# Writing the padding rows of four stored arrays at other places in the kernel

## Chip, cores and metric

The kernel runs on one core of a Trainium2 chip. The metric is the time of one execution on the device in microseconds (us), taken as the median of several runs; lower is better. Before the change it is 1056.62 us, the median of three runs (1054.39, 1056.62 and 1062.56).

## What is computed

Four graph layers on 2708 nodes with 512 features each; every layer adds its result to its input and normalises the rows. `adj` is a sparse 2708 x 2708 matrix whose first nodes have many neighbours and whose later ones have few. Cut to what matters:

```
# layer 0
d = 1 / sqrt((adj + I).sum(1))
x = layernorm(x + (d[:, None] * (adj + I) * d[None, :]) @ x @ W.T + b)
# layer 1
mask = adj > 0;  head = mask / max(sqrt(row sum of mask), 1e-12);  inc = adj + head
x = layernorm(x + (inc @ x) / row sum of inc)
# layer 2 (adj is both adj_a and adj_b)
h = x @ W_sa;  e = exp(-leaky_relu(s_left + s_right)) where adj != 0, else 0
x_a = (e / (row sum of e + 1e-5)) @ h;  x_b = adj @ (x @ W_gcnb) + b_gcnb
x = layernorm(x + sigmoid(attn_a * x_a + attn_b * x_b))
# layer 3
x = layernorm(x + relu(adj @ (max(sign(x), 0) @ sign(weight).T)))
```

## The kernel before

**Blocks and tiles.** The 2708 rows are cut into 22 blocks of 128 (the last has 20). Block 0, the dense one, is multiplied with all 22 blocks of the matrix. For every other block b the kernel first searches which nodes are its neighbours and packs them into `ROOM[b]` tiles of 128 (107 tiles over all blocks). A list of node numbers, `index[b]`, goes with each tile. A place in a tile that no neighbour fills points to a row behind the real ones: the arrays in device memory have `PAD + P` rows with `PAD = N = 2708`, and rows `PAD` and up must hold zeros.

**Stored arrays.** `y_rows` (layer 0's projected features), `x1_rows` (output of layer 0), `x2_rows` (output of layer 1, the product h, and two score columns; 1026 numbers per row) and `xw_rows` (the sign product, in half precision) live in device memory. Each layer gathers rows of one of them with indirect DMAs that POOL issues: `gathered` (L582, its DMA at L584) and, in layer 2, `gathered_2` (L1723). The score column of the padding rows of `x2_rows` holds a very large number (`MASKED`, 1e30), so that its exponential is zero. In the profile both `x1_rows` and `x2_rows` appear as `x_rows`.

**The start.** The pool `pre` (from L669) holds what only the search needs. SP loads the rows of two blocks (`load`, L685: two halves `arow` from `adj`, four buffers; `load_x`, L693: x and a column of the transposed matrix). Then come ACT's DMAs in this order: the weight `w0` (L703), the padding rows of the four arrays (L708), the second half of the padding rows of `x2_rows` (L712) and the two mask columns (L718). `zero` is a 128 x 128 tile; each padding DMA reads it four times, so that a row of 512 numbers is written in four pieces of 128. POOL makes small constants.

**The search.** `turn(at)` (L1182) takes one block at a time, in the order of the groups `GROUPS`: (1), (2, 3), (4, 5), (6, 7, 8) and so on, and block 0 last. In a turn, ACT sums the rows (`sum_rows`, L761), DVE marks non-zeros (`mark`, L806), PE counts them, and for each complete group DVE, PE and ACT make the list (`count`, `steps_of`, `look_up` with the cast `steps` at L931, `keep_looked` with the copy `look` at L963, `list_nodes` ending at L993 with `row_at`). `fetch` (L1012) then has POOL gather the group's matrix tiles, one indirect DMA for each of 107 tiles (L1014); between some of them a POOL memset `rest` (L1020) lets time pass. Two turns behind, `scale0` (L1052) scales a block of `y` and stores it to `y_rows` on ACT's queue (L1057). In turn `NTURN` (22, after the last block) `count_block0` (L1165) counts block 0's positive entries.

The turns stand inside `with in_order()` (L591, used at L1235): it makes each engine run the instructions traced within it in the order in which they are written. Elsewhere the order on an engine is chosen at build time.

**Layer 0.** The loop at L1401 takes the blocks in `sequence` (0, 1, 21, 2, ..., 20): gathers from `y_rows` (L584 by L1411), products on PE (`add_tile`, its matmul at L1318), a normalisation, and a store to `x1_rows` by SP (L1430). After a turn it runs what the table `between` (L1379) lists for it: loads and columns for layer 2's attention, the signs of the last weight (`signs`, L1352, which loads `w3` on ACT's queue at L1354), counts and roots for layer 1. Layers 1 to 3 follow with gathers from `x1_rows`, `x2_rows` and `xw_rows`.

Of the kernel before, what the change touches and what calls it, by code (L numbers as in the profile page):

```python
# [8 lines left out]
F32 = mybir.dt.float32  # L9
F32R = mybir.dt.float32r  # L10
BF16 = mybir.dt.bfloat16
F16 = mybir.dt.float16
# [7 lines left out]
P = 128  # L20
# [4 lines left out]
MASKED = 1e30  # L25
# [470 lines left out]
def sparse_layers(ctx, tc, x, adj, adj_t, w0_t, b0, w_sa, a_sa, w_gcnb, b_gcnb, wa, ba, wb, bb, w3_t,  # L496
# [11 lines left out]
    nc = tc.nc  # L508
    N, D = x.shape
    KC = D // P  # L510
    NB = -(-N // P)
    PAD = N
    XW = 2 * D + 2
# [12 lines left out]
    const = ctx.enter_context(tc.tile_pool(name="s_const", bufs=1))  # L526
# [18 lines left out]
    y_rows = dram.tile([PAD + P, D], F32, tag="y_rows", name="y_rows")  # L545
    x1_rows = dram.tile([PAD + P, D], F32, tag="x1_rows", name="x1_rows")
    x2_rows = dram.tile([PAD + P, XW], F32, tag="x2_rows", name="x2_rows")
    xw_rows = dram.tile([PAD + P, D], F16, tag="xw_rows", name="xw_rows")
# [24 lines left out]
    dia_pos = const.tile([P, NB], F32, name="s_dia_pos")  # L573
    own0 = const.tile([P, NB], F32, name="s_own0")
    own1 = const.tile([P, NB], F32, name="s_own1")
    head0_row = const.tile([P, P], F32, name="s_head0_row")
    cols = const.tile([P, NB, EXTRA], F32, name="s_cols")

# [90 lines left out]
    with tc.tile_pool(name="s_pre", bufs=1) as pre:  # L669
# [31 lines left out]
            load_x(b)  # L701
        w0 = pre.tile([P, KC, D], F32, name="s_w0")
        nc.scalar.dma_start(w0, w0_t.rearrange("(k p) o -> p k o", p=P))  # L703
        zero = pre.tile([P, D], F32, tag="y", name="s_zero", bufs=3)[:, :P]
        nc.vector.memset(zero, 0.0)
        for d in (y_rows, x1_rows, x2_rows, xw_rows):
            z = zero.bitcast(F16)[:, :P] if d is xw_rows else zero
            nc.scalar.dma_start(  # L708
                d[PAD:, :D].rearrange("p (k i) -> p k i", i=P),
                z[:, None, :].to_broadcast([P, KC, P]),  # L710
            )
        nc.scalar.dma_start(  # L712
            x2_rows[PAD:, D : 2 * D].rearrange("p (k i) -> p k i", i=P),
            zero[:, None, :].to_broadcast([P, KC, P]),
        )
        masked = pre.tile([P, XW - 2 * D], F32, name="s_masked")
        nc.vector.memset(masked, MASKED)
        nc.scalar.dma_start(x2_rows[PAD:, 2 * D :], masked)  # L718

        tri = pre.tile([P, P], F32, name="s_tri")  # L720
        nc.vector.memset(tri, 1.0)
# [65 lines left out]
        def inverse_root(b: int):  # L787
            m = rows(b)
            deg, root_ = degree_of.pop(b)
            return newton_steps(  # L790
                dinv[:m, b : b + 1], deg[:m], root_[:m, 0:1], root_[:m, 1:2], 1
            )
# [76 lines left out]
        def count(g):  # L869
            b0_, G = g[0], len(g)  # L870
            hit = small.tile([P, GM, NB, 2], BF16, tag="hit", name=f"hit{b0_}", bufs=2)
            nc.vector.tensor_scalar(
                hit[:, :G], search[g]["hits"][:, :, :, 0:2], 0.0, None, op0=ALU.is_gt
            )
            kind = small.tile([P, 3, GM * NB], BF16, tag="kind", name=f"kind{b0_}", bufs=2)
            upper, both, lower = (kind[:, c, : G * NB] for c in range(3))
            side = [hit[:, :G, :, c].rearrange("p g s -> p (g s)") for c in range(2)]
            nc.vector.tensor_tensor(both, side[0], side[1], op=ALU.mult)
            nc.vector.tensor_tensor(upper, side[0], both, op=ALU.subtract)
            nc.vector.tensor_tensor(lower, side[1], both, op=ALU.subtract)  # L880
            turn = small.tile([P, 3, GM * NB], F32, tag="turn", name=f"turn{b0_}", bufs=2)
            for c in range(3):
                nc.vector.tensor_tensor_scan(
                    turn[:, c, : G * NB], keep[:, :G].rearrange("p g s -> p (g s)"),
                    kind[:, c, : G * NB], 0.0, op0=ALU.mult, op1=ALU.add,
                )
            turns = turn[:, :, : G * NB].rearrange("p c (g s) -> p c g s", g=G)
            nc.vector.tensor_copy(found[:, :, b0_ : b0_ + G], turns[:, :, :, NB - 1])
            table = small.tile([P, 3 * GM, NT], BF16, tag="table", name=f"table{b0_}", bufs=2)
            nc.vector.tensor_tensor(  # L890
                table[:, : 3 * G, :NB].rearrange("p (c g) s -> p c g s", c=3), turns,
                kind[:, :, : G * NB].rearrange("p c (g s) -> p c g s", g=G), op=ALU.mult,
            )
            nc.vector.tensor_copy(table[:, : 3 * G, NB + 2], lane[:, : 3 * G])
            search[g].update(table=table)
# [269 lines left out]
        def count_block0():  # L1165

            for h, ar in enumerate(arows.pop(0)):
                nc.vector.tensor_scalar(
                    ar, ar, 0.0, 0.0, op0=ALU.is_gt, op1=ALU.add, accum_out=counts0[:, h : h + 1]
                )  # L1170
# [7 lines left out]
        def each(action, at: int):  # L1178
            if 0 <= at < NTURN:
                action(arrival[at])  # L1180

        def turn(at: int):  # L1182
            step_of = {at - last_at[g]: g for g in GROUPS[1:]}

            def chain(action, since: int):
                if step_of.get(since, SOON) != SOON:
                    action(step_of[since])

            each(degree, at - 1)
            each(root, at - 1)  # L1190
            each(own_diagonal, at - 1)
            chain(steps_of, 2)
            each(sum_rows, at)
            steps = inverse_root(arrival[at - 1]) if 0 < at <= NTURN else []
            found_in = step_of.get(1)

            def count_found():
                count(found_in)
                count_partitions(found_in)

            if found_in:
                steps.insert(0, count_found)
            if at < NTURN and arrival[at]:
                mark(arrival[at], steps)
            else:
                for step_ in steps:
                    step_()
            if found_in == SOON:
                steps_of(SOON)
            each(load_x, at + 2)  # L1210
            each(load, at + 2)
            each(transpose_x, at)
            each(keep_transposed, at)
            chain(look_up, 2)
            chain(list_nodes, 3)
            if found_in == SOON:
                look_up(SOON)
                keep_looked(SOON)
            if at == 0:
                for step_ in (  # L1220
                    count, count_partitions, steps_of, look_up, keep_looked, list_nodes
                ):
                    step_(GROUPS[0])
            each(scale0, at - 2)
            each(project0, at - 1)
            chain(keep_looked, 2)
            each(fold, at - 3)
            each(grow0, at - 3)
            if found_in == SOON:
                list_nodes(SOON)  # L1230
            fetch(len(to_fetch))
            if at == NTURN:
                count_block0()

        with in_order():  # L1235
            for at in range(NTURN + 4):
                turn(at)
# [87 lines left out]
    with tc.tile_pool(name="s_l0", bufs=10, reuse_waits="tile") as lp:  # L1325
# [14 lines left out]
        def attention_columns(s: int):  # L1340
            for k in range(KC):
                scr = lp.tile([P, D], F32, tag="scr", name=f"scr{s}_{k}", bufs=1)
                nc.vector.scalar_tensor_tensor(
                    scr, wsa[:, k, :D], 1.0, a_row[:, s, :], op0=ALU.mult, op1=ALU.mult,
                    accum_out=vec[:, s, k : k + 1],
                )
# [5 lines left out]
        def signs(k: int):  # L1352
            w3 = work.tile([P, D], F32, tag="xb", name=f"s_w3_{k}")
            nc.scalar.dma_start(w3, w3_t[k * P : (k + 1) * P, :])  # L1354
            neg = lp.tile([P, D], F32, tag="scr", name=f"s_neg{k}", bufs=1)
            nc.vector.tensor_scalar(neg, w3, 0.0, None, op0=ALU.is_lt)
            nc.vector.scalar_tensor_tensor(
                bw[:, k, :], w3, 0.0, neg, op0=ALU.is_gt, op1=ALU.subtract
            )
# [4 lines left out]
        def grow1(j: int):  # L1364
# [12 lines left out]
            grown1.append(j)  # L1377

        between = {  # L1379
            2: [attention_loads], 4: [lambda: attention_columns(0)],  # L1380
            5: [lambda: attention_columns(1)], 6: [attention_sides],
            8: [lambda: signs(0)], 10: [lambda: signs(1)], 12: [lambda: signs(2)],
            14: [lambda: signs(3)],
        }
# [124 lines left out]
    with tc.tile_pool(name="s_l1", bufs=8, reuse_waits="tile") as lp:  # L1509
# [67 lines left out]
        for at, b in enumerate(sequence):  # L1577
            m = rows(b)
            if b:
# [8 lines left out]
                for i0, n, (r0, r1) in runs_of(b, 3):  # L1588
# [4 lines left out]
                        name=f"inc{b}_{i0}", bufs=4 if half else 3,  # L1593
# [323 lines left out]
    with tc.tile_pool(name="s_l3", bufs=11, reuse_waits="tile") as lp, \  # L1917
# [92 lines left out]
        for at, b in enumerate(order3):  # L2010
# [21 lines left out]
            for i0 in range(0, tiles(b), CH3):  # L2032
                n = min(CH3, tiles(b) - i0)
                p = halves_of(
                    packed[b][:, i0 : i0 + n, :].rearrange("p n i -> p (n i)"), P, n * m,
                    f"{b}_{i0}",
                )
# [94 lines left out]
```

## Time and profile before

The profiled execution took 1000.5 us; its span, from the first instruction to the last, is 998.8 us. The median of the runs shown is 1056.62 us.

| engine | busy us | share of the span | instructions |
|---|---|---|---|
| PE (matmul) | 875.6 | 88% | 3775 |
| DVE | 657.8 | 66% | 2571 |
| POOL | 549.6 | 55% | 580 |
| PEld (weight load) | 458.8 | 46% | 3793 |
| ACT | 386.5 | 39% | 821 |

By stretch, from the busy times of each engine in each:

| us from the start | PE busy | DVE busy | ACT busy | POOL busy | DMA share | GB/s |
|---|---|---|---|---|---|---|
| 0 to 12 | 1.45 | 4.80 | 0.00 | 2.79 | 0.85 | 276 |
| 12 to 24 | 2.50 | 4.68 | 6.54 | 0.00 | 1.11 | 262 |
| 24 to 44 | 16.01 | 15.77 | 12.21 | 13.24 | 1.03 | 388 |
| 100 to 140 | 37.51 | 38.17 | 26.74 | 34.41 | 0.98 | 332 |
| 140 to 165 | 23.89 | 23.23 | 12.60 | 20.94 | 0.50 | 149 |
| 165 to 195 | 7.21 | 14.68 | 1.45 | 23.00 | 0.53 | 146 |
| 240 to 260 | 18.93 | 13.49 | 0.88 | 15.43 | 0.79 | 243 |

How to read it: the busy columns are microseconds within the stretch. The DMA share is the mean busy share of the core's 16 DMA engines, counted by their packets, so that it can pass 1. DMA-issuing instructions do not count as busy; in a timeline they stand under the queue of the engine that issues them (ACTq, SPq). L708 is line 708 of the kernel. A wait is named by the engine that waited and by what ended last before it went on.

### The profile page before, as it was taken

How to read it: one execution, taken by the hardware profiler on the slowest of the kernel's cores; microseconds unless marked ns; L12 is line 12 of the kernel's file. 1: busy time of each engine (PE TensorE's matmuls, PEld its weight loads, DVE VectorE, ACT ScalarE, POOL GpSimd, SP SyncE). 2: the span in 40 equal slices, each digit the busy share in tenths (PEclk: the TensorE clock that was granted, in tenths of full speed). 3: DMA queues.
4: the chain of work that ended last, by engine and by line, in shares of the span. 5: the costliest groups of instructions: out<-in, count | busy, mean ns of one | idle time of the engine just before them, and what ended most of it. 6: DMA issues, size and time to landing. Idle time of an engine off the chain costs nothing.

```text
span 998.8 us, 13107 instructions
## 1 busy us (share of the span) xinstructions
PE 875.6 (88%) x3775; PEld 458.8 (46%) x3793; DVE 657.8 (66%) x2571; ACT 386.5 (39%) x821; POOL 549.6 (55%) x580
## 2 busy tenths in 40 slices
PE   1899997198999889999999989988989999789993
PEld 1555553022233244555555533444545555458872
DVE  4889998235677745555554356666768777647776
ACT  3667672000000125544444333333334333246564
POOL 1688888777777367645332154434343333057773
PEclk9999999599999999999999999999999999979998
DMA  9999984477778577766544476768487566289997
GB/s 275 351 360 363 359 273 118 131 217 230 243 248 256 157 223 217 225 186 207 190 138 126 138 265 242 249 225 273 156 264 231 191 200 209 86 248 340 356 262 230
DMA packets 96294, 231.16 MB, mean 231 GB/s; under 512 B 14204, under 2 KB 27884, under 8 KB 96212
## 3 DMA queue, kind: packets, MB, share of 16 engines
q0 software_dynamic: 46896, 139.22, 46.3%
q1 hardware_dynamic: 37368, 76.25, 22.2%
q10 hardware_dynamic: 11948, 14.76, 4.6%
q8 instruction: 32, 0.52, 0.2%
q14 instruction: 50, 0.41, 0.1%
HBM read 188.51 MB, written 31.71 MB: 220 GB/s over the span
## 4 chain that ended last, share of the span: by engine, by line
PE 53%; DMA 20%; DVE 16%; issue 4%; ACT 3%; POOL 3%; ACTq 0%; POOLq 0%; DVEq 0%; SPq 0%
PE l L1318 11%; DMA xg<-x_rows,i 10%; PE h L1535 8%; DMA xg<-y_rows,i 7%; PE l L2001 5%; PE a L1746 4%; PE e L1746 4%; PE l L2040 3%; PE y L1047 3%; PE pg L1798 2%; DVE s_mask L828 2%; PE pc L1798 2%; PE e L1568 2%; PE a L1569 2%; POOL xg L584 1%
## 5 line engine op out<-in xcount | busy, mean ns | idle before, releaser
L1723 POOL DMA_INDIRECT xg<-x_rows,i x107 | 105.3, 984 | 170.3 <-PE a L1746 39.9
L584 POOL DMA_INDIRECT xg<-x_rows,i x107 | 103.7, 969 | 95.8 <-PE l L1318 60.7
L1014 POOL DMA_INDIRECT a<-in_adj_t_dram,row_at x107 | 115.9, 1083 | 52.2 <-issue 24.9
L584 POOL DMA_INDIRECT xg<-y_rows,i x107 | 105.9, 989 | 32.6 <-issue 13.1
L1318 PE MATMUL l<-xg,a 128*64 128x512 f32 (+1 forms) x214 | 99.8, 628 | 27.2 <-DMA xg<-y_rows,i 26.5
L584 POOL DMA_INDIRECT xg<-xw_rows,i x76 | 79.0, 1039 | 31.2 <-issue 12.9
L1746 PE MATMUL a<-xg,a 128*64 128x512 f32 (+1 forms) x214 | 92.8, 603 | 3.3 <-DMA xg<-x_rows,i 3.3
L1746 PE MATMUL e<-xg,ae 128*64 128x512 f32 (+1 forms) x214 | 90.3, 603 | 3.1 <-ACT ae L1496 2.9
L1047 PE MATMUL y<-s_w,xt 128*128 128x512 f32 (+1 forms) x176 | 83.6, 620 | 0.0
L1535 PE MATMUL h<-s_wsa,xt 128*128 128x256 f32 (+3 forms) x352 | 82.0, 386 | 0.1
L1318 PE MATMUL l<-xg,inc 128*64 128x512 f32 (+1 forms) x214 | 78.0, 604 | 3.0 <-DMA xg<-x_rows,i 3.0
L1535 PEld LDWEIGHTS h<-s_wsa,xt 128*128 128x128 f32 (+1 forms) x352 | 63.9, 186 | 25.7 <-ACT xt L1530 9.9
L1491 ACT ACTIVATE ae<-sl,xg 128x64 f32<-128x64 f32 (+1 forms) x107 | 37.6, 360 | 98.4 <-DMA xg<-x_rows,i 90.4
L1318 PEld LDWEIGHTS l<-xg,a 128*64 128x64 f32 (+1 forms) x214 | 24.6, 153 | 81.3 <-DMA xg<-y_rows,i 61.0
L765 ACT ACTIVATE unused<-arow 128x1408 uint8<-128x1408 f32 (+3 forms) x44 | 58.4, 1326 | 3.2 <-DMA x_rows<-s_zero 2.4
L1426 DVE SCALAR_TENSOR_TENSOR t<-l,s_dinv,f 128x512 f32<-128x512 f32 (+1 forms) x21 | 15.7, 749 | 55.6 <-PE l L1318 55.6
L613 ACT ACTIVATE rsqs<-mv 128x1 f32<-128x1 f32 (+2 forms) x56 | 11.3, 202 | 100.3 <-DVE mv L642 95.6
L2001 PE MATMUL l<-ws,pw 128*128 128x512 f32 (+1 forms) x210 | 50.1, 392 | 0.0
L1492 DVE SCALAR_TENSOR_TENSOR ae<-ae 128x128 f32<-128x128 f32 (+5 forms) x56 | 19.3, 344 | 45.1 <-ACT ae L1491 44.8
L1047 PEld LDWEIGHTS y<-s_w,xt 128*128 128x128 f32 (+1 forms) x176 | 32.5, 195 | 34.5 <-issue 34.4
L1798 PE MATMUL pg<-s_wg,pt 128*128 128x256 f32 (+1 forms) x176 | 44.6, 391 | 3.0 <-ACT pt L1786 3.0
L638 DVE BATCH_NORM_STATS2 st<-t 128x6 f32<-128x512 f32 (+1 forms) x66 | 45.2, 685 | 0.2
(302 smaller groups left out, 1813.6 us busy)
## 6 DMA issues: line engine op xcount, KB each, us to landing
arow<-in_adj_dram SPq DMA_DIRECT2D x21, 704.0 KB
arow<-in_adj_dram SPq DMA_DIRECT2D x21, 650.0 KB
x_rows<-f SPq DMA_DIRECT2D x41, 256.0 KB
aw<-in_adj_t_dram SPq DMA_DIRECT2D x21, 320.0 KB
f<-in_x_dram SPq DMA_DIRECT2D x20, 256.0 KB
y_rows<-yt ACTq DMA_DIRECT2D x20, 256.0 KB
out_dram<-f SPq DMA_DIRECT2D x20, 256.0 KB
x_rows<-h SPq DMA_DIRECT2D x19, 257.0 KB
```

What stands on the lines that cost most here:

```text
L584: nc.gpsimd.indirect_dma_start(out=t, out_offset=None, in_=src[:, :], in_offset=bass.IndirectOffsetOnAxis(ap=index[b][:, i : i + 1], axis=0),)
L638: nc.vector.bn_stats(st[:m], t[:m])
L765: nc.scalar.activation(unused[:m, : ar.shape[1]], ar, AF.Copy, accum_out=row_sums[:m, b, h : h + 1])
L1014: nc.gpsimd.indirect_dma_start(out=packed[b][:, t + len(direct(b)), :], out_offset=None, in_=adj_t, in_offset=bass.IndirectOffsetOnAxis(ap ...
L1047: nc.tensor.matmul(ps[:m], xt[:, k, :m], w0[:, k, :], start=(k == 0), stop=(k == KC - 1))
L1318: nc.tensor.matmul(ps[r0:r1], weights, moving, start=(i == order[0]), stop=all(span(b, j) != (r0, r1) for j in order[order.index(i) + 1 :] ...
L1491: nc.scalar.activation(ev[:, i, :], sl, AF.Identity, bias=score)
L1535: nc.tensor.matmul(ps, xt[:, k, :m], w[:, k, :], start=(k == 0), stop=(k == KC - 1))
L1723: nc.gpsimd.indirect_dma_start(out=g, out_offset=None, in_=x2_rows[:, :], in_offset=bass.IndirectOffsetOnAxis(ap=index[b][:, t : t + 1], a ...
L1746: nc.tensor.matmul(ps[r0:r1], weights, moving, start=(i == order[0]), stop=all(span(b, k) != (r0, r1) for k in order[order.index(i) + 1 :] ...
L1798: nc.tensor.matmul(ps, pt[:, k, :m], w[:, k, :], start=(k == 0), stop=(k == KC - 1))
L2001: nc.tensor.matmul(whole[b], p[:r, h, b * P : (b + 1) * P], g[:r, :], start=(j == 0 and h == 0), stop=(j == NB - 1 and h == 1),)
```

## The change

The tiles `zero` (now 128 x 128 in its own right) and `masked` move from the search's pool to the pool of constants. A helper `pad_row` writes the padding rows of 512 columns of one array, on ACT's queue as before. The six DMAs leave the start. The one for `y_rows` is issued in the search's turn 22, after `count_block0` and inside the hand-written order. The other five become entries of layer 0's table `between`: `x1_rows` after turn 1, the two halves of `x2_rows` after turns 7 and 9, the mask columns after turn 11, `xw_rows` after turn 13. The data that they write and the sizes of the DMAs stay the same.

```diff
--- before.py
+++ after.py
@@ -573,6 +573,17 @@
     dia_pos = const.tile([P, NB], F32, name="s_dia_pos")
     own0 = const.tile([P, NB], F32, name="s_own0")
     own1 = const.tile([P, NB], F32, name="s_own1")
+    zero = const.tile([P, P], F32, name="s_zero")
+    nc.vector.memset(zero, 0.0)
+    masked = const.tile([P, XW - 2 * D], F32, name="s_masked")
+    nc.vector.memset(masked, MASKED)
+
+    def pad_row(d, z, c0: int = 0):
+        nc.scalar.dma_start(
+            d[PAD:, c0 : c0 + D].rearrange("p (k i) -> p k i", i=P),
+            z[:, None, :].to_broadcast([P, KC, P]),
+        )
+
     head0_row = const.tile([P, P], F32, name="s_head0_row")
     cols = const.tile([P, NB, EXTRA], F32, name="s_cols")
 
@@ -701,21 +712,6 @@
             load_x(b)
         w0 = pre.tile([P, KC, D], F32, name="s_w0")
         nc.scalar.dma_start(w0, w0_t.rearrange("(k p) o -> p k o", p=P))
-        zero = pre.tile([P, D], F32, tag="y", name="s_zero", bufs=3)[:, :P]
-        nc.vector.memset(zero, 0.0)
-        for d in (y_rows, x1_rows, x2_rows, xw_rows):
-            z = zero.bitcast(F16)[:, :P] if d is xw_rows else zero
-            nc.scalar.dma_start(
-                d[PAD:, :D].rearrange("p (k i) -> p k i", i=P),
-                z[:, None, :].to_broadcast([P, KC, P]),
-            )
-        nc.scalar.dma_start(
-            x2_rows[PAD:, D : 2 * D].rearrange("p (k i) -> p k i", i=P),
-            zero[:, None, :].to_broadcast([P, KC, P]),
-        )
-        masked = pre.tile([P, XW - 2 * D], F32, name="s_masked")
-        nc.vector.memset(masked, MASKED)
-        nc.scalar.dma_start(x2_rows[PAD:, 2 * D :], masked)
 
         tri = pre.tile([P, P], F32, name="s_tri")
         nc.vector.memset(tri, 1.0)
@@ -1231,6 +1227,7 @@
             fetch(len(to_fetch))
             if at == NTURN:
                 count_block0()
+                pad_row(y_rows, zero)
 
         with in_order():
             for at in range(NTURN + 4):
@@ -1377,8 +1374,12 @@
             grown1.append(j)
 
         between = {
+            1: [lambda: pad_row(x1_rows, zero)],
             2: [attention_loads], 4: [lambda: attention_columns(0)],
             5: [lambda: attention_columns(1)], 6: [attention_sides],
+            7: [lambda: pad_row(x2_rows, zero)], 9: [lambda: pad_row(x2_rows, zero, D)],
+            11: [lambda: nc.scalar.dma_start(x2_rows[PAD:, 2 * D :], masked)],
+            13: [lambda: pad_row(xw_rows, zero.bitcast(F16)[:, :P])],
             8: [lambda: signs(0)], 10: [lambda: signs(1)], 12: [lambda: signs(2)],
             14: [lambda: signs(3)],
         }
```

## The prediction

> **What bounds the kernel now.** I read the busy table, the chain of waits, the waits of POOL by stretch, and then ACT's instructions in order of time. PE is 88% busy over the span, but the change touches the first 45 us and layer 0, so I ask what sets the pace there. POOL's waits (engine, line, releaser, us in total, times, longest), first for 24 to 60 us, then for 60 to 100 us:
>
> ```profile
> POOL a L1014 <- DVE deg L773: 20.6, 1, 20.6
> POOL a L1014 <- DVE find L864: 5.4, 1, 5.4
> POOL a L1014 <- issue: 3.7, 16, 0.3
> ...
> POOL a L1014 <- issue: 5.8, 25, 0.3
> ```
>
> POOL begins its fetches at 24.05 us, when the list of block 1 is made (list finished at 23.58 plus 0.17), runs dry once for 5.4 us until the list of blocks 2 and 3 (44.14 plus 0.17), and starts again at 44.58. From there its waits are the 0.3 us between two DMA issues: fetches of about 1.25 us each run back to back to 195.70, then layer 0's gathers, also back to back, to about 336 us. PE is busy only 7.21 of the 30 us from 165 to 195, so POOL holds the end of the search and the start of layer 0. The later lists come before POOL needs them: blocks 4 and 5 are listed at 65.88 and fetched from 70.21 (4.3 us in hand), the next groups have 6 us, then 16 and 21. So a microsecond won or lost **before the second list at 44 us** moves everything to 336 us, and then the PE-bound rest; one lost later in the search is covered by what is in hand.
>
> What sets that list? ACT in order of time (start, duration, queue, line; in brackets the idle time and its releaser):
>
> ```profile
> 1.51 0.62 ACTq L708 DMA_DIRECT2D y_rows<-s_zero  x1
> 2.16 4.93 ACTq L708 DMA_DIRECT2D x_rows<-s_zero  x2
> 7.13 2.01 ACTq L708 DMA_DIRECT2D xw_rows<-s_zero  x1
> 9.58 1.65 ACTq L712 DMA_DIRECT2D x_rows<-s_zero  x1
> 12.06 0.34 ACTq L718 DMA_DIRECT2D x_rows<-s_masked  x1
> 12.43 1.28 ACT L765 ACT_TABLE_LOAD   x1 [12.43 <-DVE turn L883]
> ...
> 17.23 0.35 ACTq L1354 DMA_DIRECT2D s_w<-in_w_t_dram  x1
> 17.63 1.29 ACT L765 ACTIVATE unused<-arow 128x1300 uint8<-128x1300 f32 x1 [2.44 <-DMA x_rows<-s_zero]
> ...
> 20.98 0.34 ACTq L1354 DMA_DIRECT2D s_w<-in_w_t_dram  x1
> 21.36 0.35 ACT L963 COPY look<-looked 128x225 f32<-128x225 f32 x1 [1.73 <-DMA x_rows<-s_masked]
> ```
>
> See two things. The pads hold ACT's queue until 12.4 us, though DVE could already use the first half of block 1's row at 5.70. And **L1354 is a load that the code puts in layer 0**, in turns 8 and 10 of that layer's loop; it is issued at 17 and 21 us, inside the search. So outside the order written by hand (the search turns) an instruction that waits for no data or buffer is pulled forward into the first gap on its engine. b0_row (L1331), whose buffer lies in the search's memory, stays at 167.83.
>
> One more view, SP's waits:
>
> ```profile
> SPq L690 <- DMA s_w<-in_w_t_dram: 7.9, 1, 7.9
> ```
>
> Block 2's row has a free buffer, yet its load waits until 11.1 us for w0 to land. The waits fit one rule: counting SP's and ACT's DMAs together in issue order, each waits for the one eight places earlier. That is my reading of the waits, not something a row states.
>
> [...] the DMA share is 0.99 from 5 to 10 us with both queues at work. [...] to 30 us SP's queue moves 5.88 MB in 61.0% of the 16 engines' time (10.4% per MB), ACT's, with the pads, 2.75 MB in 37.7% (13.7% per MB). [...] `look` stood 1.73 us behind a DMA that it does not use.
>
> **The change part by part.**
>
> *Price of a pad.* ACT's 2.75 MB to 30 us are w0 and two w3 pieces (1.57 MB, at SP's 10.4% per MB: 16%) and the pads (1.18 MB, the remaining 21%). 21% of 30 us is 6.4 us of all DMA engines, or 1.4 us for a pad of 256 KB. Issue times on ACT: 0.62 us on an empty queue, 1.0 to 3.9 on a full one.
>
> *The memsets* of zero (0.17 us) and masked (0.06) stay on DVE at the start, ahead of its first data at 5.70: nothing. If that cover were gone they would cost 0.2 us.
>
> *The pad of y_rows* is inside the hand-written order, so it does move, to turn 22 behind the search. There ACT waits 3.55 us (163.1 to 166.6) and the DMA share is 0.50 to 0.53; its issue costs 0.6 to 3.9 us and is covered. What queues behind it is the root at 166.63, the last `y` scaling and its y_rows store. The first gather of y_rows is at 195.70, 29 us after that store, because POOL is still fetching. Taken at nothing; if that cover were gone, about 4 us. At the start it frees 0.6 us of ACT and 1.4 us of DMA.
>
> *The pads of x1, x2 (two), the masks and xw* are in layer 0's between-list, exactly where L1354 is. They need only the two constants, and nobody has written their rows. I expect them to be pulled forward as L1354 was: first x1, x2, the two L1354 loads and the second x2 pad, by their order in the code, into the 11 us before ACT's first data. Then the same DMAs stand ahead of the search in another order, SP's second row still waits for w0 at about 11 us, and only two things change: the y pad is gone (1.4 us of DMA), and L1354 no longer stands before `unused` and `look` (2.44 and 1.73 us), though a late pad may take its place there. Between 0 and 5 us won; I take **2 us**.
>
> *The layer 0 side.* With the pads pulled forward nothing is added there. Otherwise five issues of 0.3 to 3.9 us and 5.0 us of DMA (6.4 less the y pad) fall in a stage where ACT is busy 0.5 to 1.9 of each 20 us and the DMA share is 0.73 to 0.83: covered, bound 0 to 3 us. SP's and POOL's order does not change.
>
> Sum: 1000.5 us of the profiled execution (span 998.8) minus 2 gives 998.5. The median shown, 1056.6, is 56.1 us above that execution, and the profile has no row for it; queue and transfer time should carry over unscaled: **1054.6 us**.
>
> **Rivals.**
>
> *The pads stay where they are written.* Then ACT is free at about 1.5 us and SP's second row need not wait for w0. The cast `steps` (19.38) could run at 15.3, just after `table` (15.1): 4.1 us, and `look` loses its wait, where 0.8 us is left (21.36 against looked's end at 20.2, less the copy gap). Lists come about 5 us earlier by this path, and by at most the 6.4 us of DMA time, the share being about 1.0 to 100 us. Less up to 3 in layer 0: 3 to 8 won, taken at 6: 1050.6 us. For it: the diff's words. Against it: L1354.
>
> *The pads land inside the search on ACT.* If they are pulled into gaps between ACT's search steps instead of ahead of them, each is a full-queue issue (up to 3.9 us) and a wait like L1354's (1.7 to 2.4), with row sums, `steps` and `look` behind it and DVE, PE and POOL behind those. Five times 4 is 20 us; of what falls after 44 us the first 4.3 is in hand, and the 12 us that pads hold at the start now is saved. It decides against the change when more than 10 us are lost net, which takes most of the pads on the path. Taken at +12: 1068.6 us. Against it: the gap ahead of the first data holds six pads today.
>
> *The order elsewhere shifts.* A different start can re-sort instructions in the layers, either way by some us; no row prices it.
>
> **How the numbers follow.** Pulled forward ahead of the search 0.62 (its own range 1051 to 1059); staying put 0.20; inside the search 0.12; re-sorted order 0.06. A measurement of this kernel can tell about 1% (10.6 us) from no change; the three runs shown spread over 8.2. Faster by over 1%: a third of the second case and a little of the last, 0.08. Slower: most of the third and a third of the last, 0.13. Within: 0.79. For 8 in 10 the range takes the first two cases with the spread of the runs, and stops short of the third: 1045 to 1065.
>
> **What would show it.** In the changed kernel, look at ACT to 30 us: x1's pad and L1354 there confirm the pulling forward; pads at 210 us and later refute it. ACT's table load near 11 to 12.4 us, POOL's first fetch at 20 to 24 and its restart at 40 to 44.6 confirm the 2 us; a restart near 38 is the first rival, above 50 the second. POOL's first gather should come at 195.7 us less the shift of that restart. The y pad should stand near 163 us with nobody waiting for it. I am wrong if POOL is found dry between 50 and 190 us, or if the layers' spans change by more than the start does.

## The result and the profile after

| | median us (range, runs) | ratio to before, 95% interval |
|---|---|---|
| before | 1064.26 (1054.39 to 1074.41, 22) | |
| after | 1070.47 (1058.59 to 1081.86, 22) | 1.0053 [1.003, 1.0077] |

The change made the kernel about 6 us slower: within the 1% that the forecast called the same, but of the other sign than the 2 us forecast as won, and above the range. A ratio leaves out runs over 1.5% above the fastest of their kernel, so it can differ a little from the quotient of the medians. The profiled execution after took 1069.84 us (span 1067.9). It can't be laid beside the profile shown of before: that one had a mean granted TensorE clock of 0.968, this one 0.932. A second profile of the kernel before, taken at 0.932 (`b1` below, span 1062.6), serves as its partner.

PE, POOL and SP run their instructions in the same order as before, and on DVE one small instruction has moved. Only ACT's order differs: at the start, and by the y pad after the search. So the cause lies in the first 50 us, in the y pad, in the constants' new place in memory, or in what the DMAs wait for.

ACT in order of time in the changed kernel (start, duration, queue or engine, line; in brackets the idle time and its releaser). L582 is now `pad_row`, L1351 the load of `w3`, L1381 the masks, L761 the row sums of `sum_rows` (the second sum of a block takes the second half of its row):

```profile
0.80 0.48 ACTq L714 DMA_DIRECT2D s_w<-in_w_t_dram  x1
1.51 0.61 ACTq L582 DMA_DIRECT2D x_rows<-s_zero  x1
...
5.74 1.38 ACT L761 ACTIVATE unused<-arow 128x1408 uint8<-128x1408 f32 x1 [2.30 <-DMA arow<-in_adj_dram]
5.75 0.38 ACTq L582 DMA_DIRECT2D x_rows<-s_zero  x1
...
14.94 0.37 ACTq L582 DMA_DIRECT2D x_rows<-s_zero  x1
15.40 0.24 ACT L927 CAST steps<-find 128x100 bf16<-128x100 f32 x1 [3.08 <-DVE after L939]
15.43 0.44 ACTq L1351 DMA_DIRECT2D s_w<-in_w_t_dram  x1
16.23 0.35 ACT L959 COPY look<-looked 128x225 f32<-128x225 f32 x1 [0.59 <-PE looked L949]
20.42 0.34 ACTq L1381 DMA_DIRECT2D x_rows<-s_masked  x1
21.18 0.52 ACTq L582 DMA_DIRECT2D xw_rows<-s_zero  x1
21.73 1.28 ACT L780 ACT_TABLE_LOAD   x1 [5.15 <-DMA f<-in_x_dram]
23.03 0.20 ACT L780 ACTIVATE root<-deg 128x1 f32<-128x1 f32 x1
23.14 1.36 ACT L761 ACTIVATE unused<-arow 128x1408 uint8<-128x1408 f32 x1
...
32.49 1.29 ACT L761 ACTIVATE unused<-arow 128x1300 uint8<-128x1300 f32 x1 [1.39 <-DMA arow<-in_adj_dram]
```

All five pads were pulled forward, as L1354 was before. But only x1's stands ahead of the first row sum. The others lie between ACT's search steps, up to 21.7 us. The masks are issued 3.8 us after `look` ended (16.58), with nothing else between, and ACT's next step waits behind them and the xw pad: `root` at 23.03 and the first row sum of block 2 at 23.14.

SP's waits to 32 us and then SP in order of time (L701 is `load`, two halves of a row; L707 the column of `load_x`):

```profile
SPq L701 <- DMA s_w<-in_w_t_dram: 7.1, 2, 6.9
SPq L707 <- DMA x_rows<-s_zero: 6.5, 1, 6.5
```

```profile
3.10 7.82 SPq L701 DMA_DIRECT2D arow<-in_adj_dram  x2
...
12.04 0.45 SPq L706 DMA_DIRECT2D f<-in_x_dram  x1
18.96 0.33 SPq L707 DMA_DIRECT2D a<-in_adj_t_dram  x1
19.62 8.17 SPq L701 DMA_DIRECT2D arow<-in_adj_dram  x2
```

The same loads of block 3 in `b1`:

```profile
20.98 0.43 SPq L696 DMA_DIRECT2D a<-in_adj_t_dram  x1
21.53 1.05 SPq L690 DMA_DIRECT2D arow<-in_adj_dram  x2
```

In the changed kernel the first pair is block 2's: its first half goes out at 3.10 (11.12 in `b1`), its second waits for w0, as was forecast for the whole row. New is the rest: block 3's column load waits 6.5 us for a pad of `x_rows`, which it does not use, and the two halves of block 3's row take from 19.62 to 27.79 to be issued, where `b1` took from 21.53 to 22.58.

POOL's waits from 24 to 60, and then from 60 to 100 us:

```profile
POOL a L1010 <- DVE find L860: 14.6, 1, 14.6
...
POOL a L1010 <- DVE s_own L1060: 5.9, 2, 5.6
```

The first fetch begins at 18.91 us, 5 us earlier than before. The dry spell behind it has grown to 14.6 us (5.4 in the profile of before, 8.8 in `b1`), and the restart is at 47.5, against 47.05 in `b1`. In later profiles of the changed kernel it came at 51.0 and 50.22. The 5.9 us in the second stretch show POOL dry once more; in `b1` its waits for data there are 0.7 us.

### The profile page after: what moved, and what is told of

Its sections match the earlier page's. It is cut to its first block, busy times and chain, and to the rows that moved or that the text cites. A ratio compares the mean times of both kernels' runs of the same rounds, so it can differ in the third digit from the quotient of the medians.

```text
span 1067.9 us, 13124 instructions
## 1 busy us (share of the span) xinstructions
PE 907.8 (85%) x3793; PEld 469.2 (44%) x3793; DVE 654.7 (61%) x2571; ACT 384.6 (36%) x821; POOL 549.3 (51%) x580
## 4 chain that ended last, share of the span: by engine, by line
PE 56%; DMA 14%; DVE 13%; issue 6%; ACT 5%; another core or an unknown queue 5%; POOL 1%; ACTq 0%; POOLq 0%; SPq 0%; DVEq 0%
PE l L1315 15%; DMA xg<-x_rows,i 10%; PE h L1536 7%; PE l L2002 4%; PE a L1747 4%; PE e L1747 4%; PE y L1043 3%; PE l L2041 3%; PE pg L1799 2%; PE l L1370 2%; DMA arow<-in_adj_dram 2%; PE pc L1799 2%; ACT unused L761 2%; PE e L1569 1%
## 5 line engine op out<-in xcount | busy, mean ns | idle before, releaser
L1747 PE MATMUL a<-xg,a 128*64 128x512 f32 (+1 forms) x214 | 95.1, 616 | 4.7 <-DMA xg<-x_rows,i 4.7
L595 POOL DMA_INDIRECT xg<-xw_rows,i x76 | 77.8, 1024 | 39.6 <-issue 18.4
L1043 PE MATMUL y<-s_w,xt 128*128 128x512 f32 (+1 forms) x176 | 96.1, 697 | 0.0
L1747 PE MATMUL e<-xg,ae 128*64 128x512 f32 (+1 forms) x214 | 92.8, 619 | 3.7 <-ACT ae L1497 3.5
L1315 PE MATMUL l<-xg,inc 128*64 128x512 f32 (+1 forms) x214 | 80.2, 616 | 1.7 <-DMA xg<-x_rows,i 1.1
L761 ACT ACTIVATE unused<-arow 128x1408 uint8<-128x1408 f32 (+3 forms) x44 | 58.3, 1325 | 8.4 <-DMA arow<-in_adj_dram 7.8
L1043 PEld LDWEIGHTS y<-s_w,xt 128*128 128x128 f32 (+1 forms) x176 | 36.9, 221 | 42.7 <-issue 42.7
L2041 PE MATMUL l<-xg,p 128*128 128x512 f32 (+1 forms) x152 | 41.1, 417 | 11.1 <-DVE p L1930 10.6
L1543 DVE COPY h<-h 128x260 f32<-128x260 f32 (+1 forms) x20 | 8.6, 428 | 63.6 <-PE h L1536 40.3
```

What stands on the lines that cost most here:

```text
L595: nc.gpsimd.indirect_dma_start(out=t, out_offset=None, in_=src[:, :], in_offset=bass.IndirectOffsetOnAxis(ap=index[b][:, i : i + 1], axis=0),)
L761: nc.scalar.activation(unused[:m, : ar.shape[1]], ar, AF.Copy, accum_out=row_sums[:m, b, h : h + 1])
L1043: nc.tensor.matmul(ps[:m], xt[:, k, :m], w0[:, k, :], start=(k == 0), stop=(k == KC - 1))
L1315: nc.tensor.matmul(ps[r0:r1], weights, moving, start=(i == order[0]), stop=all(span(b, j) != (r0, r1) for j in order[order.index(i) + 1 :] ...
L1747: nc.tensor.matmul(ps[r0:r1], weights, moving, start=(i == order[0]), stop=all(span(b, k) != (r0, r1) for k in order[order.index(i) + 1 :] ...
L2041: nc.tensor.matmul(ps[:m], p[:, h, i * m : (i + 1) * m], src[i0 + i], start=False, stop=(i0 + i == len(src) - 1 and h == 1),)
```

## Experiments

All times are compared with the kernel before on the same chip and in the same set of runs. The first set ran on chip 11 (before: 1071.29 us), the third on chip 13 (1064.93 us, and 1074.47 us when part of it was run again), all at a granted clock of about 0.93 to 0.94; the second ran on chip 14 at about 0.965 (1004.73 us). Diffs are against the changed kernel.

### First set: which part of the change

**b1** is the kernel before, unchanged.

> The kernel before, unchanged, for its profile beside the others. Both theories: ratio 1.000 within 0.3%; span near 1060 us at a granted clock of about 0.935 as in the runs of the changed kernel, not the 998.8 us at 0.968 of the profile that the prediction read. If so, POOL is no longer saturated from 44 us on: it should run dry in the search, as it does in the profile of the changed kernel (5.6 us in 60 to 100, 6.8 in 160 to 200).

0.999 [0.9966, 1.0013]. First list at 23.56 us, second at 46.61.

**const_only** keeps the new helper and constants, with all pads at the start:

```diff
+        pad_row(y_rows, zero)
+        pad_row(x1_rows, zero)
...
+        nc.scalar.dma_start(x2_rows[PAD:, 2 * D :], masked)
-                pad_row(y_rows, zero)
-            1: [lambda: pad_row(x1_rows, zero)],
...
```

> The two constants in the pool of constants, all six pad DMAs at the head in the order of before. Theory A (SP's row loads wait at the start for pads that share their completion counter) and theory B (the pad of y_rows behind the search holds up its end): 1.000. Theory C (other memory addresses): 1.005.

1.0019 [0.9982, 1.0056]: no cost of the constants' new home is seen. The interval still reaches the change's loss; y_both below, which has the constants in the same place, narrows it with 1.0005 [0.9991, 1.002].

**y_only** moves only the y pad to turn 22; the others stay at the start. **rest_only** does the reverse.

> Only the pad of y_rows moves behind the search; the other five stay at the head in the order of before. A: 0.997 to 1.000, since the start is relieved of one pad and no pad comes between the row loads. B: 1.005. In the profile block 3's second half row is issued near 22 us for A.

> The pad of y_rows stays at the head, the other five are in layer 0's table as in the change. A: 1.004 to 1.008, with block 3's second half row issued at 26 us or later and the second list 3 us or more later than in the run of before. B: 1.000.

y_only: 1.0069 [1.0041, 1.0097]; rest_only: 1.0004 [0.9975, 1.0032]. So the y pad's move, which the forecast took at nothing, seemed to cost it all. Theory A, that pads put among SP's row loads hold them up, missed in both runs.

### Second set: the late place or the missing early one

**y_both** issues the y pad at the start and again in turn 22. **y_mid** is y_only with the pad in turn 8. **pinned** is the change with its five other pads held in layer 0: each is tied behind the last ACT instruction of its turn. **clean_start** holds the `w3` loads in layer 0 too and leaves the y pad at the start.

```diff
+    @contextmanager
+    def in_place():
+        ins = next(i for i in reversed(nc.cur_bb.bb.instructions)
+                   if i.engine == mybir.EngineType.Activation)
+        with tc.issue_after(ins):
+            yield
...
-            1: [lambda: pad_row(x1_rows, zero)],
+            1: [placed(lambda: pad_row(x1_rows, zero))],
...
```

> All six pads at the head as before, and the pad of y_rows a second time in turn 22 (the same zeros again). Theory B (that DMA behind the search holds up its end): 1.004 to 1.008 against before. Theory D (what costs is the missing pad at the head: the DMAs that follow share their completion counters in another pairing, and the first loads of SP wait longer): 0.998 to 1.002.

> As y_only, but the pad of y_rows is issued in turn 8, in the middle of the search, where nothing of layer 0 is near. B: 0.997 to 1.001, with no pad near the end of the search. D: 1.004 to 1.008, first list near 26 to 27 us as in y_only against 24 in before.

> The change with its five pads tied to the places where they are written (each issued behind the last ACT instruction of its turn), so that the start has only the weight load and two w3 pieces; the pad of y_rows in turn 22. The first rival of the prediction: 0.994, with the second list 5 us earlier than in before. B: 1.000 or slower, since that pad's cost stays. If the search makes its own pace after the start, no gain whatever the start does: 0.998 to 1.003.

> As pinned, but the pad of y_rows at the head and the w3 loads tied to their places too. B and the first rival: 0.993 to 0.996, faster than pinned by the cost of the late pad. D: like pinned. The order of layer 0's instructions changes in some places on PE and DVE, which no theory prices (0.3% either way).

| kernel | ratio | second list, us |
|---|---|---|
| before (profile shown) | | 44.14 |
| y_both | 1.0005 [0.9991, 1.002] | 45.02 |
| y_mid | 1.004 [1.002, 1.0059] | 46.47 |
| pinned | 0.9952 [0.9933, 0.9971] | 38.85 |
| clean_start | 0.9976 [0.9959, 0.9994] | 38.76 |

y_both shows that the late pad is free, as forecast; y_mid that its late place doesn't matter. What costs time is that a DMA is *missing* at the start; whether the DMA itself counts or its 256 KB, the third set tells. ACT at the start of pinned (L777 are the row sums):

```profile
5.38 1.38 ACT L777 ACTIVATE unused<-arow 128x1408 uint8<-128x1408 f32 x1 [2.23 <-DMA arow<-in_adj_dram]
...
14.67 0.24 ACT L943 CAST steps<-find 128x100 bf16<-128x100 f32 x1 [2.56 <-PE find L936]
15.58 0.35 ACT L975 COPY look<-looked 128x225 f32<-128x225 f32 x1 [0.67 <-PE looked L965]
15.95 1.28 ACT L796 ACT_TABLE_LOAD   x1
18.07 0.20 ACT L796 ACTIVATE root<-deg 128x1 f32<-128x1 f32 x1 [0.84 <-DVE deg L785]
18.18 1.36 ACT L777 ACTIVATE unused<-arow 128x1408 uint8<-128x1408 f32 x1
```

With no pad in the search the table load follows `look` at once (5.15 us later in the changed kernel), and block 2's first row sum starts at 18.18 instead of 23.14. clean_start has the same early lists but wins less; its order of instructions in layers 0 and 1 differs at many places from before (about 200 places of PE's order hold another instruction, against 6 in pinned), so the rest of it can't be read.

### What the DMAs wait for

The trace writes beside each DMA the completion counter that its landing raises, and beside an issue the counters that it waits for. In the profiles of before and of the changed kernel the first 24 DMAs of SP and ACT raise eight counters (100 and 102 to 108 before; 100, 102 to 104 and 106 to 109 in the change), each of them three times. Put in the order of these numbers, with each queue in its own order, they are three rounds of the eight, so that the previous user of a counter stands eight places earlier. For 27 of the DMAs the two traces tell when the previous user landed: none of the 27 was issued before that, and 12 were issued 0.02 us after it. The forecast had read this from the waits as a rule of eight places. That every other run keeps it was not shown. Some of the pairs, in the changed kernel (all numbers in us) and, as far as the waits show them, in after_tiny2, the same kernel with one more small DMA (next set):

| load or pad | in the change it waits for | which lands at | issued at | in after_tiny2 its wait ends with | issued at |
|---|---|---|---|---|---|
| block 3's column (SP) | first x2 pad | 18.95 | 18.96 | a pad of `x_rows` | 18.23 |
| block 3's second half (SP) | second x2 pad | not told | 27.46 | no pad | by 22.70 |
| second x2 pad (ACT) | x1 pad | 14.92 | 14.94 | not told | 14.93 |
| masks (ACT) | block 2's second half | 20.40 | 20.42 | a `w3` load | 18.47 |
| xw pad (ACT) | block 2's x | 21.16 | 21.18 | no wait behind the masks | 18.84 |

### Third set: shift the pairing

If the pairing makes the loss, one DMA of 512 bytes that shifts it must undo it, though no pad goes back to its old place. **after_tiny** is the change with this line behind w0; **y_tiny** is y_only with the same line where the y pad stood; **a1** is the change again; **pinned_yhead** is pinned with the y pad at the start. In y_tiny nothing else in the order of any engine differs from y_only. In after_tiny the build also moved two ACT steps ahead of the DMA beside them (`steps` before the second x2 pad, `look` before the second `w3` load) and one DVE copy by one place.

```diff
+        nc.scalar.dma_start(y_rows[PAD : PAD + 1, :P], zero[:1, :])
```

> The changed kernel again, beside the others. Its start holds SP's third row behind the second x2 pad, so its second list should be 1 to 3 us later than in before, and the ratio 1.002 to 1.006. On a chip that grants the higher clock (near 0.967) POOL is saturated after the second list, and the loss should equal the delay of that list.

> y_only with a DMA of 512 bytes (one padding row's first quarter, zeros) where the y pad stood at the head, so that the later DMAs share completion counters as in before, without the 256 KB. Theory E (the pairing of the counters makes the loss): 0.997 to 1.000, first list at or before 24 us. Theory F (without those 256 KB the row loads come sooner and starve the other pads, and who waits for those): 1.004 as in y_only, first list at 25 us or later.

> The change with the same DMA of 512 bytes behind the weight load. E: the waits for counters fall on other DMAs, and the ratio leaves the change's 1.005 (0.995 to 1.002 if block 3's row no longer stands behind a pad). F: 1.005.

> As pinned (0.9952), but the pad of y_rows at the head. If a late y pad costs something once the start is clean: faster than pinned. If not, as fast or slower by what one pad costs at the start (1.4 us of DMA): 0.995 to 0.998.

a1: 1.0062 [1.0037, 1.0087]; after_tiny: 0.9971 [0.9941, 1.0]; pinned_yhead: 0.9954 [0.9932, 0.9975]. But y_tiny: 1.0047 [1.0011, 1.0082], with a second list as early as 43.60 us. This spoke against the pairing, though the medians put it at 1065.82 against 1064.93 us, 0.08% more. So four kernels were run again, side by side.

> The y pad in turn 22, the other pads at the head, and a DMA of 512 bytes where the y pad stood. If a late start is all that the missing head pad costs, this kernel's start is as early as the one before (second list within 1 us of 44 to 46.6 or earlier) and the ratio is 0.997 to 1.001; the 1.0047 measured once was then chance. If something that no list shows goes with the missing pad, the ratio is again 1.003 to 1.006 with an early second list.

> The y pad alone moved to turn 22. Late start: first list about 3 us later than before, second 1.5 to 4 us later, ratio 1.004 to 1.008. Should the ratio of this kernel and that with the small DMA be equal, the pairing of the completion counters isn't what the y pad's move costs.

> The change with a DMA of 512 bytes behind w0. Pairing of the counters: second list 2 us or more earlier than before, ratio 0.995 to 0.999. If the pads' place on ACT inside the search costs the time, the ratio is that of the change, 1.004 to 1.007.

> The change itself beside the three others. Second list 0.4 to 4 us later than before, block 3's second half issued after 27 us or its row held to 21 us, ratio 1.004 to 1.007.

y_tiny2: 0.9985 [0.995, 1.002] against y_only2: 1.0091 [1.0048, 1.0133]; after_tiny2: 0.9948 [0.9926, 0.997] against a2: 1.0064 [1.0035, 1.0092]. Side by side, one small DMA takes back 1.1% in each pair; y_tiny's first value was not repeated. The later half of the program is no explanation: y_both also has one DMA more from turn 22 on, and its ratio is 1.0005.

SP in order of time in a2:

```profile
20.94 0.33 SPq L707 DMA_DIRECT2D a<-in_adj_t_dram  x1
21.48 7.45 SPq L701 DMA_DIRECT2D arow<-in_adj_dram  x2
```

SP's waits in a2, to 32 us:

```profile
SPq L707 <- DMA x_rows<-s_zero: 8.3, 1, 8.3
SPq L701 <- DMA s_w<-in_w_t_dram: 7.1, 1, 7.1
SPq L701 <- DMA x_rows<-s_zero: 6.7, 1, 6.7
```

SP in after_tiny2:

```profile
18.23 0.33 SPq L707 DMA_DIRECT2D a<-in_adj_t_dram  x1
18.69 4.01 SPq L701 DMA_DIRECT2D arow<-in_adj_dram  x2
```

In a2 block 3's row itself waits 6.7 us for a pad and is issued by 28.93; in after_tiny2 by 22.70. ACT in a2, then in after_tiny2, around the masks:

```profile
15.97 0.35 ACT L959 COPY look<-looked 128x225 f32<-128x225 f32 x1 [0.68 <-PE looked L949]
22.59 0.34 ACTq L1381 DMA_DIRECT2D x_rows<-s_masked  x1
24.66 0.52 ACTq L582 DMA_DIRECT2D xw_rows<-s_zero  x1
25.21 1.28 ACT L780 ACT_TABLE_LOAD   x1 [8.89 <-DMA f<-in_x_dram]
```

```profile
15.84 0.35 ACT L960 COPY look<-looked 128x225 f32<-128x225 f32 x1 [0.67 <-PE looked L950]
15.85 0.34 ACTq L1352 DMA_DIRECT2D s_w<-in_w_t_dram  x1
18.47 0.33 ACTq L1382 DMA_DIRECT2D x_rows<-s_masked  x1
18.84 0.52 ACTq L582 DMA_DIRECT2D xw_rows<-s_zero  x1
19.39 1.28 ACT L781 ACT_TABLE_LOAD   x1 [3.21 <-DMA s_w<-in_w_t_dram]
```

`look` ends at nearly the same time (16.32 and 16.19 us). Then ACT is idle 8.89 us in one kernel and 3.21 in the other, in front of a table load that needs neither pad. The masks have another partner. The wait in front of the table load ends with a load of x in a2, for which the xw pad waited until 24.66 us, and with a `w3` load in after_tiny2. In both the table load begins 0.03 us after the xw pad's issue has ended (25.18 and 19.36 us): it did not pass the DMAs that waited ahead of it.

The y pad's move alone is undone by the same small DMA, but its waits are others. ACT in y_only2 (L1356 loads `w3`, L766 sums), then in y_tiny (L1357, L767):

```profile
12.28 1.38 ACT L766 ACTIVATE unused<-arow 128x1408 uint8<-128x1408 f32 x1
...
20.83 0.35 ACTq L1356 DMA_DIRECT2D s_w<-in_w_t_dram  x1
21.23 1.29 ACT L766 ACTIVATE unused<-arow 128x1300 uint8<-128x1300 f32 x1 [7.48 <-DMA x_rows<-s_zero]
```

```profile
16.61 0.35 ACTq L1357 DMA_DIRECT2D s_w<-in_w_t_dram  x1
17.00 1.29 ACT L767 ACTIVATE unused<-arow 128x1300 uint8<-128x1300 f32 x1 [1.50 <-DMA x_rows<-s_zero]
```

In y_only2 ACT does begin 1.45 us sooner than before (13.73). But the `w3` load holds the second half's sum for 7.48 us (2.44 in the profile of before). Its wait ends with a pad of `x_rows` in all three kernels (before, the first x2 pad lands at 17.21 us and the load goes at 17.23); what differs is when: the load goes at 20.83 us in y_only2 and at 16.61 in y_tiny. SP's waits did change their partners: block 2's column load now waits 8.4 us for the xw pad. Why the pad lands late in y_only2 is not shown by a wait. To 32 us SP's row loads wait 0.5 us for pads of `x_rows` there, 2.9 before and 10.1 in y_tiny; with less of them held back they may take the DMA engines from the pad, which is an estimate from these waits, not shown by a run.

### One number for all of them

The second list follows the last row sum of block 3. When ACT starts that sum, in each kernel's profile:

| kernel | start, us | ratio |
|---|---|---|
| pinned | 24.49 | 0.9952 |
| clean_start | 24.75 | 0.9976 |
| pinned_yhead | 25.12 | 0.9954 |
| after_tiny, after_tiny2 | 27.38, 27.65 | 0.9971, 0.9948 |
| y_tiny (profile of its first run) | 29.63 | 1.0047, again 0.9985 |
| const_only, b1, before | 30.21, 30.25, 30.27 | 1.0019, 0.999, 1 |
| y_both | 30.79 | 1.0005 |
| rest_only | 31.07 | 1.0004 |
| y_mid | 32.01 | 1.004 |
| y_only2, y_only | 32.72, 33.32 | 1.0091, 1.0069 |
| after, a2, a1 | 32.49, 34.54, 35.53 | 1.0053, 1.0064, 1.0062 |

All kernels under 27.7 us are faster than before (after_tiny's interval just reaches 1.0), all over 32 us slower, and those from 30.2 to 31.1 the same. y_tiny's first ratio is the only one out of line.

## Why the prediction was wrong, and where it was right

**Right: the pulling forward.** All five pads left the table `between` for the first 22 us, and the diff's words about layer 0 didn't come true.

**Right: the late y pad.** In the changed kernel it has its place on ACT at 195.86 us:

```profile
195.84 0.18 ACT L959 COPY look<-looked 128x25 f32<-128x25 f32 x1 [0.61 <-ACT yt L1052]
195.86 0.54 ACTq L582 DMA_DIRECT2D y_rows<-s_zero  x1
```

It follows at once on the `look` before it, and the first gather of `y_rows` comes 14 us later, at 210.3. y_both prices it: 1.0005.

**Right: what is at stake before the second list.** Pads truly in layer 0, the first rival, were forecast to bring lists about 5 us earlier and 6 us in all. pinned measured a second list 5.3 us earlier (44.14 to 38.85) and 0.48% of 1004.73, or 4.8 us, with 2.9 to 6.7 by its interval. One part of that rival didn't hold: SP's second half of block 2's row still waits 7.1 us for w0 in pinned.

**Wrong: "Then the same DMAs stand ahead of the search in another order".** This is the step that failed. Two things in it did not hold. The pads did not stay ahead of the search: they were put between ACT's search steps, four of five behind the first row sum. That is the second rival's place, and its mechanism, held steps on ACT, is in the trace: 5.15 us idle behind `look`, 8.89 in a2. The place alone does not make the loss: rest_only and after_tiny have their pads between these steps too, at 1.0004 and 0.9971. And a reordering is not neutral where, as here, DMAs wait on the one eight places earlier. The forecast stated that rule, used it for w0 and block 2's row, and did not carry it through a new order. With the order that came, it puts block 3's column behind the first x2 pad and block 3's second half behind the second one: 6.5 us of waiting on SP in the changed kernel, 8.3 and then 6.7 in a2. Of this the second rival saw only ACT's half.

**Mis-sized: the second rival.** It was taken at +12 us with a chance of 0.12; the change cost 0.53% of 1064, or 5.6 us. No issue of a pad took over 0.61 us in the changed kernel (up to 3.85 before, which the forecast had put down to a full queue; no run shows that cause). Its five waits of 4 us each don't add up on the path: x1's pad and the first x2 pad cost nothing there, and early starts give some of the rest back (block 2's first half 8 us earlier, first list at 18.4 instead of 23.6).

**Wrong: "the y pad is gone" as a pure gain of 1.4 us.** ACT did start 1.45 us earlier in y_only2; that this is close to the forecast's 1.4 us is chance, since those are time of the DMA engines. But the missing DMA shifted the pairing of those behind it, and y_only lost 0.7 to 0.9%. The forecast left out this larger term.

**Off: the level.** The sum hung on the median of three runs, 1056.62; 22 runs gave 1064.26. Of the 15.9 us between forecast and result 7.6 are this, the other 8.2 the sign of the effect. The 56 us for which the forecast had no row may be of the kind that separates the sets of runs here (1004.73 us on chip 14, 1064 to 1074 elsewhere); that was not tested. The statement that POOL runs without a gap from 44.58 us on also belongs to the higher clock: in b1 its fetches start within 0.5 us of several later lists (list and fetch at 93.23 and 93.68, 143.89 and 144.34, 191.27 and 191.71), so less is in hand there than the forecast counted.

**What stays open.** The path from the late row sum to the end is shown by medians, not in one pair of profiles. At the lower clock single profiles of one order of instructions differ by more than the effect: the last fetch is at 207.9 us in b1 and at 218.0 in const_only. At the higher clock pinned keeps 5.0 of its 5.3 us to the last fetch and 3.4 to layer 1's first gather; y_mid keeps only 0.6 of 2.3 us to the last fetch, too little for the 3 us that its median lost. How ACT's held queue and SP's held loads share the loss wasn't separated either; the small DMA relieves both. rest_only gives a hint: ACT is idle 4.92 us behind `look` there, nearly as long as in the change, but block 3's row is issued by 20.42 us instead of 27.79, and its ratio is 1.0004.

**A better version.** pinned (0.9952) and pinned_yhead (0.9954) are about 0.5% faster than the kernel before; after_tiny (0.9971 and 0.9948) comes near them without holding anything in place.

## To carry to other kernels

Where an instruction waits for no data and stands outside a hand-written order, its place in the source is no promise (five DMAs written in layer 0 were issued by 21.7 us here): say what it must follow, or look where it went. In the profiles of before and of the change SP's and ACT's DMAs share eight completion counters. Before one of them is added, dropped or moved, pair each with the one that used its counter before it, here eight places earlier; a load on the critical path should not be paired with a write that lands late (block 3's two loads waited 8.3 and 6.7 us for pads in a2). Adding one tiny DMA that shifts the pairing tells a loss of this kind from others (512 bytes took back 1.1% here).

## What was not expected of the hardware

- A DMA of 512 bytes took as long as its surroundings. In after_tiny2 it was issued at 1.51 us behind w0 on the same queue; block 2's x load waited 4.3 us for it and was issued at 10.34 us. ACT's second row sum, behind a pad issued at 10.66, waited 3.97 us for w0.
- Pads of 256 KB land late among row loads: in the changed kernel the first x2 pad was issued at 5.75 us and landed at 18.95; in a2 the second x2 pad was issued at 14.58 us, and SP's load of block 3's second half waited 6.7 us for it; it was issued by 28.93. The forecast's price, 1.4 us of DMA time for a pad, says nothing of when it lands.
- The same kernel took 1004.73 us on a chip with a granted clock of about 0.965 and 1064 to 1074 us at 0.93 to 0.94: 6 to 7% of time beside about 3% of clock. On chip 13 alone its median went from 1064.93 to 1074.47 us between two sets. What makes these differences was not tested.
